# Four column tiles of 32 in place of two of 64 in the query and output products of a cross-attention kernel

## The chip, the cores and the metric

The kernel runs on one core of a Trainium2 chip. The metric is the device time of one execution in microseconds. Before the change it is 565.37 us, the median of three runs (564.01, 565.37, 566.51).

## The reference

Eight sequences of 256 tokens with 1024 features attend to eight contexts of 256 tokens, with 32 heads of 32 features. All data is 32-bit floating point.

```
x  = (hidden - mean) * rsqrt(var + 1e-5) * gamma + beta
Q  = split_heads(x @ Wq.T)
K  = V = split_heads(ctx)
scores = where(mask, Q K^T / sqrt(32), -inf)
attn   = merge_heads(softmax(scores) V)
out    = hidden + attn @ Wout.T
```

## The kernel before, in words

The program is written out in full, with no loop on the chip: a fixed order for each engine. It goes through 64 passes (n = 0 to 63), one for each sequence and each group of four heads (128 of the 1024 features). A pass does these things on TensorE, in this order:

- the scores of the next pass, line 494: eight tiles of the array, 32 rows by 64 columns each, with 256 moving columns
- some steps of the output product of an earlier sequence
- the product of probabilities and values of the pass before the last, line 645: eight tiles of 64 rows by 32 columns, with 128 moving columns
- more steps of the output product, and the query product of a later pass or sequence.

Meanwhile VectorE, ScalarE and GpSimd work on the softmax and the transposes of a pass, and the transfers are issued by SyncE's queue.

The query product and the output product are the two large ones (1024 x 1024 weights). For the first two sequences the query product is made directly, in `make_q` and `first_q`: eight chunks of 128 features added up in PSUM, with 257, 256, 129 or 128 moving columns. For the other six, and for the output product, the kernel uses a scheme with seven products of half-size blocks, from sums and differences of blocks, instead of eight. `query_product` makes one of the seven query products of a sequence in one pass: 4 x 4 chunks with 128 moving columns. `product_steps` makes one chunk after another of the seven output products, with 512 moving columns, as the table of steps for each pass says; `end_steps` does so for the last sequence.

All of them go through the helper `product` (line 216 in the profile). It takes one chunk, a stationary operand of 128 x 128 and a moving operand of 128 rows, and issues it as two matmuls on two column tiles of the array, each with 64 columns of the stationary operand, the same moving operand and its own 64 partitions of the PSUM tile. Both tiles use all 128 rows.

An fp32 matmul of the program stands as two matmuls and two weight loads in the trace: a query product of 16 chunks, 32 matmuls of the program, is a block of 64 matmuls with 64 weight loads there. The tiles' names are pq (query product), po (output product), sc (scores) and pv (values). `K` is 32 and `NA` is 4, the number of such tiles in 128 partitions.

Of the kernel before, what the change touches and what calls it, by code (L numbers as in the profile page):

```python
# [51 lines left out]
P = 128  # L52
# [7 lines left out]
def xattn_kernel(  # L60
# [10 lines left out]
    nc = tc.nc  # L71
# [9 lines left out]
    K = 32  # L81
    NA = P // K
# [129 lines left out]

    def product(out, stationary, moving, **flags):

        for w in range(2):
            nc.tensor.matmul(  # L216
                out[ts(w, P // 2)], stationary[:, ts(w, P // 2)], moving, **flags
            )

    xnTs, mvs, rstds = {}, {}, {}  # L220

# [69 lines left out]
    def first_q(s, chunks=range(NC)):  # L291

        if s == 0:
            pqs[0] = ps_q.tile([P, 512], F32, tag="pq", name="pq_0")
        cols = ds(0, P) if s == 0 else ds(P, P + 1)
        for c in chunks:
            product(
                pqs[0][:, cols], wq[:, 0, c, :], xnT0[:, c, cols],
                start=(c == chunks[0]), stop=(c == chunks[-1]),
            )  # L300
        nc.scalar.activation(qa[:, 0, cols], pqs[0][:, cols], AF.Copy, scale=NEG_SCALE)  # L301
# [41 lines left out]
    def make_q(n, second=False, chunks=range(NC)):  # L343
        b, o = divmod(n, NQ)
        if chunks[0] == 0:
            if second:
                bank = ps_o.tile([P, 512], F32, tag="po", name=f"pq_{n}")
            else:
                bank = ps_q.tile([P, 512], F32, tag="pq", name=f"pq_{n}")
            pqs[n] = bank[:, : S + 1] if b == 0 else bank[:, :S]  # L350
        for c in chunks:
            product(
                pqs[n], wq[:, o, c, :], xnTs[b](c), start=(c == 0), stop=(c == NC - 1),
            )
# [89 lines left out]
    def query_product(b, p):  # L444
        name, which, begins = Q_PRODUCTS[p]
        if b == SPLIT and name == "A11":
            which = "B11"
        if begins:
            pqs[b] = ps_q.tile([P, NK, P], F32, tag="pq", name=f"pq_{b}_{name}")
        x_ = x_part(b, name)  # L450
        for o in range(NK):
            w = weights(which, o)
            for c in range(NK):
                product(
                    pqs[b][:, o, :], w[:, c], x_[:, c], start=begins and o + c == 0,
                    stop=c == NK - 1, skip_group_check=True,
                )
# [714 lines left out]
```

## Time and profile before

| what | value |
|---|---|
| median of three runs | 565.37 us |
| profiled execution, its own time | 565.4 us |
| span in the profile | 563.6 us |
| instructions in the span | 26534 |
| TensorE matmuls / weight loads | 10364 / 10364 |
| of them the products' (line 216) | 4148 / 4148 |
| granted TensorE clock | 1.00 |

PE is TensorE's matmuls and PEld its weight loads, which run beside the matmuls. DVE is VectorE, ACT is ScalarE, POOL is GpSimd, SP is SyncE. A row of a group gives line, engine and operation, the tile that is written and those read, rows and columns of the array's tile (`128*64`), the shape, the count, then busy time in us and mean time of one in ns, and the idle time of the engine just before such instructions, with what ended it. "issue" means that the profile finds nothing that the engine waited for. A row of a stretch gives its limits, its length, then for each engine the busy time with the count of instructions, the granted clock, the busy share of the transfer engines and the rate in GB/s. A row of a queue gives packets, megabytes and the share of the 16 transfer engines' time that its packets took. A row of the chain of waits gives start, length and what it was; a row of the timeline the same, with the count and, in brackets, the idle time of the engine before it.

### The profile page before, as it was taken

Reading aid. Unit: us, or ns where it says so; the run is one execution under the profiler, and the core shown is the slowest. Engines: PE = TensorE matmul, PEld = TensorE weight load, DVE = VectorE, ACT = ScalarE, POOL = GpSimd, SP = SyncE. Lnnn points to the kernel's source line nnn. Section 1 sums busy time; section 2 is a strip of 40 time slices with the busy share of each in tenths; the row PEclk is TensorE's granted clock in tenths of the full one; section 3 lists DMA queues with packets and bytes.
Section 4 is the critical chain, followed back from the end, with each engine's and each line's share of the span. In section 5 each row is a group of like instructions: output and inputs, shape, how many; then the busy total and the mean of one; then the engine's idle time right before and its main releaser. Section 6 shows DMA issues by size and latency. Waiting matters only on the chain.

```text
span 563.6 us, 26534 instructions
## 1 busy us (share of the span) xinstructions
PE 556.2 (99%) x10364; PEld 350.8 (62%) x10364; DVE 467.4 (83%) x1716; ACT 423.4 (75%) x1464; POOL 394.8 (70%) x636
## 2 busy tenths in 40 slices
PE   8999999999999999999999999998999999999997
PEld 8666664666656667566765676566765767644443
DVE  5979889999997988888898888986878878879923
ACT  3699998898768867787777977777767776869920
POOL 2688887899786675876569665776658657448780
PEclk9999999999999999999999999999999999999999
DMA  8967657966798767887779668786667874536751
GB/s 302 396 187 208 168 158 213 305 199 168 226 299 248 217 181 197 259 249 222 196 223 283 204 185 232 237 263 174 166 168 251 260 207 135 153 101 184 208 170 74
DMA packets 47244, 119.43 MB, mean 212 GB/s; under 512 B 8976, under 2 KB 9744, under 8 KB 47120
## 3 DMA queue, kind: packets, MB, share of 16 engines
q1 hardware_dynamic: 46976, 117.74, 69.8%
q8 instruction: 82, 1.34, 1.0%
q14 instruction: 42, 0.34, 0.2%
q10 hardware_dynamic: 144, 0.01, 0.0%
HBM read 66.33 MB, written 11.53 MB: 138 GB/s over the span
## 4 chain that ended last, share of the span: by engine, by line
PE 77%; DVE 6%; POOL 6%; DMA 5%; SPq 2%; issue 2%; ACT 2%; DVEq 0%; POOLq 0%
PE po_S L216 17%; PE pq_A L216 16%; PE pv L645 10%; PE sc L494 9%; PE po_A L216 8%; PE pq L216 6%; PE pq_S L216 6%; PE po_end L216 3%; DVE pT L558 2%; DMA pT<-pT 2%; DMA r<-in_x_dram 2%; ACT e L537 1%; POOL e L552 1%; DVE e L533 1%; PE po_last L216 1%
## 5 line engine op out<-in xcount | busy, mean ns | idle before, releaser
L552 POOL TENSOR_SCALAR e<-e,rden 128x256 f32<-128x256 f32 x466 | 215.4, 479 | 119.8 <-DVE rden L544 116.9
L537 ACT ACTIVATE e<-e,mn 128x256 f32<-128x256 f32 x512 | 254.1, 502 | 41.7 <-DVE mn L533 41.3
L558 DVE STREAM_TRANSPOSE pT<-e 128x512 f32<-128x512 f32 x256 | 179.0, 704 | 35.6 <-POOL e L552 26.9
L533 DVE CUSTOM_DVE_ANT_0 e<-sc,mb 128x256 f32<-128x256 f32 x512 | 185.3, 416 | 22.0 <-PE sc L494 21.4
L564 ACT COPY pc<-pT 128x512 f32<-128x512 f32 x128 | 78.9, 617 | 54.7 <-DVE pT L558 35.2
L537 ACT ACTIVATION_READ_ACCUMULATOR e<-e,mn 128x1 f32 x512 | 98.2, 192 | 0.0
L645 PE MATMUL pv<-pT,v 64*32 64x128 f32 x4096 | 74.4, 274 | 0.4 <-DMA pT<-pc 0.4
L216 PE MATMUL po_S<-wo,at 128*64 128x512 f32 x304 | 73.9, 599 | 0.0
L645 PEld LDWEIGHTS pv<-pT,v 64*32 64x32 f32 x4096 | 57.0, 105 | 26.6 <-ACT pc L564 10.8
L494 PE MATMUL sc<-k,qa 32*64 32x256 f32 x2048 | 72.1, 387 | 0.2 <-ACT qa L301 0.2
L494 PEld LDWEIGHTS sc<-k,qa 32*64 32x64 f32 x2048 | 37.6, 131 | 49.2 <-issue 33.0
L216 PE MATMUL po_A<-wo,at 128*64 128x512 f32 x256 | 58.6, 599 | 0.0
L216 PE MATMUL pq<-xnT,wq 128*64 128x256 f32 (+3 forms) x544 | 58.4, 369 | 0.0
L216 PEld LDWEIGHTS pq_A<-xnT,wq 128*64 128x64 f32 x832 | 46.6, 137 | 7.1 <-issue 5.7
L216 PE MATMUL po_S<-wo,s 128*64 128x512 f32 x208 | 49.8, 600 | 0.7 <-DVE r L771 0.7
L216 PEld LDWEIGHTS pq<-xnT,wq 128*64 128x64 f32 x544 | 36.8, 136 | 19.1 <-issue 1.7
L216 PE MATMUL pq_A<-xnT,wq 128*64 128x128 f32 x832 | 47.8, 273 | 0.0
L544 DVE RECIPROCAL rden<-den 128x2 f32<-128x2 f32 x256 | 38.3, 150 | 7.3 <-ACT e L537 6.2
L533 DVE DVE_READ_ACCUMULATOR2_ANT mn<- 128x1 f32 x512 | 42.6, 83 | 0.0
L216 PEld LDWEIGHTS po_A<-wo,at 128*64 128x64 f32 x256 | 16.9, 136 | 30.0 <-issue 28.7
L762 POOL TENSOR_TENSOR r<-r,p 128x512 f32<-128x512 f32 x24 | 30.8, 1282 | 6.8 <-DMA r<-in_x_dram 4.4
L216 PEld LDWEIGHTS po_S<-wo,at 128*64 128x64 f32 x304 | 20.3, 136 | 21.9 <-issue 21.6
(100 smaller groups left out, 646.1 us busy)
## 6 DMA issues: line engine op xcount, KB each, us to landing
v<-in_kv_dram SPq DMA_DIRECT2D x32, 512.0 KB, 4.8
pT<-pT SPq DMA_DIRECT2D x128, 128.0 KB, 3.2
pT<-pc SPq DMA_DIRECT2D x128, 128.0 KB, 4.1
ring<-kept_T SPq DMA_DIRECT2D x20, 512.0 KB
k<-in_kv_dram SPq DMA_DIRECT2D x32, 256.0 KB, 3.8
x<-in_x_dram SPq DMA_DIRECT2D x15, 512.0 KB, 5.6
r<-in_x_dram SPq DMA_DIRECT2D x28, 256.0 KB, 4.5
out_dram<-r SPq DMA_DIRECT2D x28, 256.0 KB, 2.6
```

The costliest lines, as they stand in the source:

```text
L216: nc.tensor.matmul(out[ts(w, P // 2)], stationary[:, ts(w, P // 2)], moving, **flags)
L494: nc.tensor.matmul(scs[n][j][ts(w, P // 2), s, :], qa[r, n % NQ, ds(s * P + w * P // 2, P // 2)], ks[n - n % 2][r, n % 2, :], start=True, ...
L533: nc.vector.tensor_tensor_reduce(out=e[:, s, :], in0=pss[j][:, s, :], in1=mbs[n // NQ], scale=1.0, scalar=NO_SCORE, op0=ALU.add, op1=ALU.m ...
L537: nc.scalar.activation(e[:, s, :], e[:, s, :], AF.Exp, bias=mn[:, s : s + 1], scale=-1.0, accum_out=den[:, s : s + 1],)
L544: nc.vector.reciprocal(rden, dens[j])
L552: engine.tensor_scalar(es[j][:, s, :], es[j][:, s, :], rden[:, s : s + 1], 1.0, ALU.mult, ALU.mult,)
L558: nc.vector.transpose(pT[:, :, :, j, :, :].rearrange("p a i s k -> p (a i) s k"), es[j].rearrange("p s (b t) -> p b s t", t=K),)
L564: nc.scalar.copy(pc[:, :, ts(j, 2)], pT[:, 1, :, ts(j, 2)])
L645: nc.tensor.matmul(pvs[n][r][j * HD : (j + 1) * HD], vs[n - n % 2][ts(r, 2 * K), i, ds(n % 2 * P + j * HD, HD)], pT[ts(r, 2 * K), :, i, j, ...
L762: nc.gpsimd.tensor_tensor(r, r, p1s[b], ALU.add)
```

## The change

`product` issues one chunk as four matmuls on four column tiles of 32 columns in place of two on tiles of 64. Each takes 32 columns of the stationary operand, the same moving operand of 128 rows, and writes its own 32 partitions of the same PSUM tile. The flags that start and stop the accumulation are the same. Everything that calls `product` changes with it; scores and values, which have tiles of their own, stay as they are, and nothing changes place on any engine.

```diff
     def product(out, stationary, moving, **flags):
 
-        for w in range(2):
-            nc.tensor.matmul(
-                out[ts(w, P // 2)], stationary[:, ts(w, P // 2)], moving, **flags
-            )
+        for w in range(NA):
+            nc.tensor.matmul(out[ts(w, K)], stationary[:, ts(w, K)], moving, **flags)
```

In TensorE's order around the first of the query products with half-size blocks, each row stood so before (line, instruction, tiles, rows of the output by moving columns, count as matmuls of the program):

```order
L645 MATMUL pv_1_1883<-pT_1473,v_1540 32x128
L216 MATMUL po_A_1783<-wo,at_1_1345 64x512 x2
L216 MATMUL pq_S_1918<-sx,ring 64x128 x32
L216 MATMUL po_S_2030<-wo,s_0_1856 64x512 x4
L494 MATMUL sc_0_2040<-k_1709,qa 64x256 x2
```

and stands so now:

```order
L643 MATMUL pv_1_2169<-pT_1713,v_1780 32x128
L216 MATMUL po_A_2063<-wo,at_1_1569 32x512 x4
L216 MATMUL pq_S_2206<-sx,ring 32x128 x64
L216 MATMUL po_S_2350<-wo,s_0_2142 32x512 x8
L492 MATMUL sc_0_2364<-k_1981,qa 64x256 x2
```

The order of the blocks is the same; the products' rows have half the width and twice the count, and the numbers of lines after the helper are two lower.

## The prediction

> **What bounds the kernel now.** I read the busy shares first, then the chain of waits, then the stretch of the chain around one pass.
>
> ```profile
> PE 556.2 (99%) x10364; PEld 350.8 (62%) x10364; DVE 467.4 (83%) x1716; ACT 423.4 (75%) x1464; POOL 394.8 (70%) x636
> PE 77%; DVE 6%; POOL 6%; DMA 5%; SPq 2%; issue 2%; ACT 2%; DVEq 0%; POOLq 0%
> 0.00:564.00 564.00, 411.93 (x4148) 245.60 (x4148) 1.00 0.71 212
> 310.76 1.87 PE po_S L216 x8
> 312.63 3.49 PE pq_S L216 x64
> 316.12 1.72 PE po_S L216 x8
> 317.84 1.05 PE sc L494 x32
> 318.89 1.09 PE pv L645 x64
> 319.98 0.57 PE po_S L216
> ```
>
> TensorE is busy 99% and carries the chain; the third row (the stretch view, line 216 alone: time, PE, PEld, clock 1.00) gives the products 412 of its 556 us and 4148 of its 10364 matmuls, each with one weight load. What lengthens TensorE lengthens the kernel almost one for one.
>
> The chain rows give the pace. 64 matmuls of 128 columns last 3.49 us: 109 ns for each two. Eight of 512 columns last 1.72 us: 430 ns for each two. So both column tiles stream at once, and the time is that of the columns streamed, 0.84 ns each. The value products (pv, eight tiles of 64x32) need 1.09 us for eight rounds of 128 columns with the change of array shape and the first load inside. Since 109 and 430 ns stand in the ratio of the columns, the weight loads run beside the matmuls; one can be seen only in the first round after another shape.
>
> **Part 1: does a round of four tiles cost the same?** The trace has no 128x32 tile. From below: the four tiles stream the same columns as the two, so 109 and 430 ns, and nothing is gained in the steady state. From above: the pv rows, eight tiles over four column groups, 1.09 us / 8 = 136 ns with everything in it; 27 ns in 109 is 25%, and 25% of 412 us would be +103 us. Of the 1.09 us, one shape change and load are paid once and not per round, so I take the lower bound: 0 us.
>
> **Part 2: the first load of a block.**
>
> ```profile
> L645 PEld LDWEIGHTS pv<-pT,v 64*32 64x32 f32 x4096 | 57.0, 105 | 26.6 <-ACT pc L564 10.8 <-issue 10.5 <-ACT e L537 2.7
> L216 PEld LDWEIGHTS pq_A<-xnT,wq 128*64 128x64 f32 x832 | 46.6, 137 | 7.1 <-issue 5.7 <-ACT at L658 1.1
> ```
>
> A load of 32 columns takes 105 ns, one of 64 takes 137. Products begin after another shape once in each of the 64 passes: 64 x 32 ns = -2.0 us (at least 0, if the array's other delays cover it). Against that the last tile of a round starts two tiles later than now. pv issues 128 instructions in 1.09 us, at most 8.5 ns each; two tiles more are two to four instructions, 17 to 34 ns, at the end of 64 blocks: +1.1 to +2.2 us. Parts 1 and 2 together: -1 us, between -2 and +0.2.
>
> **Part 3: the instructions themselves.** Each product matmul becomes two of half the width, with two loads: 4148 x 2 = 8296 more instructions, beside 20,728. They have to be fetched.
>
> ```profile
> q8 instruction: 82, 1.34, 1.0%
> 0.00:278.04 278.04, 275.25 (x5125) 180.95 (x5125) 241.39 (x885) 221.92 (x754) 210.46 (x317) 1.00 0.76 230
> 0.00:381.75 381.75, 378.96 (x7142) 248.88 (x7143) 332.43 (x1222) 302.92 (x1039) 282.36 (x444) 1.00 0.77 230
> 278.04 0.35 PEld L216 LDWEIGHTS po_S<-wo,s 128*64 128x64 f32 x4 [0.20 <-issue]
> 383.71 0.30 PEld L216 LDWEIGHTS pq_S<-xnT,wq 128*64 128x64 f32 x6 [1.93 <-issue]
> q8 instruction: 1, 0.02, 5.3%
> ```
>
> The first row is the queue of instruction fetches: 82 packets, 1.34 MB. That is 16 KB each, and 20,728 / 82 = 253 matmuls and loads per packet, so this queue serves TensorE. Rows two and three are stretches from the start, with the count of matmuls and loads run (PE and PEld). Rows four and five are waits of the weight loads for which the profile finds no releaser ("issue"), in the middle of product blocks. Between the two waits lie 14,285 - 10,250 = 4035 instructions, 15.96 packets: both stops are at a packet's edge. I call the instructions of one packet a page. The last row is the queue in 381.0 to 382.5, during the long wait; from 376 to 381 and from 382.5 to 384.8 it has no packet. So TensorE ran to the end of what it had, the packet was in by 382.5, and work went on 1.2 us later. At 278.04 it is the same: packet in by 276.9, resumed 1.15 us after. I take 1.3 us from landing to use (landings read to the packet).
>
> Now the turnaround: from the moment TensorE crosses one page's edge until the page after it is usable. If it is longer than the page lasts, TensorE stands still for the rest. I read it for all 82 packets (landing + 1.3 us - time at which the edge was run); the shortest, one in the middle and the longest are shown by the counts at their edges and the queue's rows for 220.4 to 221.5, 326.1 to 327.2 (the longest's is above).
>
> ```profile
> 0.00:221.83 221.83, 219.04 (x3989) 144.01 (x3991) 192.88 (x715) 179.03 (x608) 169.27 (x248) 1.00 0.75 230
> 0.00:324.95 324.95, 322.16 (x6004) 211.99 (x6006) 282.40 (x1038) 259.81 (x886) 243.44 (x376) 1.00 0.76 230
> 0.00:375.86 375.86, 373.07 (x7014) 244.72 (x7022) 327.49 (x1200) 297.03 (x1020) 279.38 (x438) 1.00 0.76 230
> q8 instruction: 1, 0.02, 5.4%
> q8 instruction: 1, 0.02, 5.5%
> 100.00:500.00 400.00, 397.57 (x7888) 261.14 (x7872) 342.11 (x1259) 306.10 (x1071) 280.76 (x463) 1.00 0.73 215
> 100.00:500.00 400.00, 300.02 (x3350) 191.66 (x3352) 1.00 0.73 215
> PE po_S L216 <- DVE r L771: 0.7, 1, 0.7
> ```
>
> Shortest 0.9 us (221.83 to 222.7: the sequencer runs ahead and had asked early), middle 3.5 us (324.95 to 328.4), longest 7.8 us (375.86 to 383.7). 16 of the 82 are over 4.5 us, with a mean of 5.8.
>
> How long does a page last? From 100 to 500 us (the rows of that stretch: all, and line 216 alone) TensorE runs 15,760 instructions in 400 us, 39.4 per us: 253 last 6.4 us. Few turnarounds are longer, and each late one must meet a short page; that is why only 2.4 us are lost now (the 1.93 and 0.20 us above, and 0.2 more). With the change, 6702 are added: 22,462 in 400 us, 56.2 per us, and a page lasts 4.5 us. Inside a query product it is worse: 64 matmuls and 64 loads in 3.49 us become 256 instructions, one whole page in 3.5 us.
>
> The sum. At 4.5 us flat, the excess of the 82 turnarounds is 16 x (5.8 - 4.5) / 82 = 0.26 us a page. The stretch holds 22,462 / 253 = 89 pages: 23 us. Pages are not alike, though: I laid the added instructions on the trace's own times, which gives 114 pages of 3.0 to 8 us, and took each length against each of the 82 turnarounds: 31 us. By the same reckoning the kernel of now would lose 4.6 us where it loses 2.4, so I scale nothing and only take off the 2.4 that are in the span already: +28 us. Nothing hides it: the waits fall on TensorE, which is the chain, and its waits for others (the largest kind is 0.7 us, the last row) are too small to absorb them. The other engines only become idler: DVE at 83% has room.
>
> Bounds of this term: with turnarounds 0.5 us shorter throughout the same sum is 20 us (18 net), with 0.5 us longer 46 us (44 net). Longer is possible, since a sequencer that has just stood still has no lead to ask early with; shorter, since a standing TensorE leaves the transfers (share 0.73) more room.
>
> The profiled execution took 565.4 us with a span of 563.6, the median of the runs is 565.37. Sum: 565.4 - 1 + 28 = 592.4, say **593 us**.
>
> **The rivals.**
> Fetches stay hidden; this one ends on the other side, no slower. Mechanism: the next packet is asked for early enough however fast the stream runs, as at 221.83, where it was in before the edge. Then parts 1 and 2 alone count: 565.4 - 1 = 564.4 us, or 563.4 with the best of part 2. For it: 2 of the 82 packets are in before their edge even now, and all stops together cost 2.4 us. Against it: 40 of the 82 turnarounds exceed the 3.5 us that a page lasts in a query product. It decides if turnarounds come out at 3 us or less nearly everywhere.
> A rule of the Trainium skill speaks for this rival: "Runtime: NRT & Kernel Launch", section "Instruction fetch mechanics", says that instructions come in 16 KiB blocks of 256, that the next is fetched while one runs, and that crossing a boundary is mostly hidden. The packets of 16 KB here agree; "mostly hidden" agrees at 6.4 us a page, but the 1.93 us at an edge does not. By that rule the end would be 564.4 us.
>
> Fetches bind throughout. Each stop takes away the lead with which the next packet is asked for. The shortest turnaround's packet moved from 220.4, 1.4 us ahead of its edge, so the lead is worth about 1 us. With every turnaround 1 us longer the same sum is 69 us, 66 net: 565.4 - 1 + 66 = 630 us. For it: the mean turnaround of 3.6 us plus 1 is over the 4.5 us of a page. Against it: the sequencer refills quickly after a stop (the packet after 383.71 was in by 385.9).
>
> Four tiles stream slower than two (read or write of four column groups with all 128 rows): up to the 136 ns of part 1, +103 us, and the fetches then hide behind the slower pace: 565.4 - 1 + 103 = 667 us. Against: pv keeps four column groups going with less than 136. That the four tiles run two by two would double 412 us and end near 975; pv's eight at once speak against it.
>
> **How the numbers follow.** The forecast, late fetches at some 10 to 55 us net, gets 0.80; fetches hidden 0.09; bound throughout 0.07; slower streaming 0.04. The range, 573 to 620 us, is the forecast with its bounds of 18 and 44 us widened by some 10 us on each side, since one execution's turnarounds stand for all; it leaves out the hidden case and the two dear ones. A measurement of this kernel tells about 0.5% (2.8 us) from no change. Slower than that: the forecast and the two dear cases, 0.91. Of the hidden case's 0.09, 0.07 is within 0.5%, and 0.02 faster, where part 2's gain is whole and the 2.4 us lost now go too.
>
> **What would show it.** Right: the instruction queue has 114 or 115 packets; the weight loads of line 216 show waits of 0.5 to 3 us with "issue" as their end, some 30 to 40 of them, most between 100 and 500 us and few after 500, where the products have 512 columns; undisturbed blocks of 128 product matmuls still last 3.49 us; loads take about 105 ns. Wrong: undisturbed product blocks that last longer (then it is the streaming), no added "issue" waits (then fetches are hidden), or waits that end on other engines.

## The result, and the profile after

The changed kernel takes 594.16 us (median of four runs, 591.32 to 604.2) against 565.94 us for the kernel before, run beside it: a ratio of 1.0455 (95% interval 1.0389 to 1.0521). It is slower by 4.5%, 28 us. The profiled execution took 593.52 us with a span of 591.2 us, 27.6 us more than the span before. (One run of the changed kernel, 604.2 us, was disturbed; the ratio is without it.)

The page of the changed kernel: busy time, the queue of instruction fetches, the chain of waits.

```profile
PE 567.4 (96%) x14512; PEld 348.4 (59%) x14512; DVE 468.5 (79%) x1716; ACT 425.4 (72%) x1464; POOL 395.3 (67%) x636
q8 instruction: 114, 1.87, 1.3%
PE 94%; issue 3%; DMA 1%; DVE 0%; POOL 0%; ACT 0%; SPq 0%; POOLq 0%
```

There are 4148 more matmuls and as many loads, and 32 more packets of instructions. VectorE, ScalarE and GpSimd do the same work in the same busy time. The chain is TensorE and "issue". The waits of TensorE's matmuls, by tile: total, times, longest.

```profile
PE pv L643 <- issue: 7.0, 7, 1.6
PE pq_S L216 <- issue: 6.1, 7, 2.3
PE pq_A L216 <- issue: 3.5, 4, 1.6
PE po_A L216 <- issue: 1.9, 2, 1.4
```

Before, the view had one such wait, of 1.7 us. It now has 21, and they strike values (pv), whose instructions the change did not touch, as well as products. These are the times for which no matmul ran at all; a stop is longer, since the matmuls under way still finish. Here is the longest, in the timeline of the changed kernel's weight loads (start, length, engine, line, what ran, and in brackets the wait ahead of it):

```profile
255.81 0.56 PEld L216 LDWEIGHTS pq_S<-xnT,wq 128*32 128x32 f32 x19
258.96 1.05 PEld L216 LDWEIGHTS pq_S<-xnT,wq 128*32 128x32 f32 x24 [2.59 <-issue]
```

Stretches of the same kernel from the start of the span that end at this stop and at three others (length, then busy time and count for matmuls, loads, VectorE, ScalarE and GpSimd, then granted clock, DMA share and GB/s):

```profile
0.00:247.24 247.24, 238.68 (x6033) 151.76 (x6033) 209.23 (x771) 192.71 (x655) 184.33 (x272) 1.00 0.74 227
0.00:256.37 256.37, 247.81 (x6287) 157.65 (x6287) 216.04 (x797) 200.59 (x680) 189.66 (x282) 1.00 0.74 226
0.00:287.03 287.03, 275.21 (x7047) 176.92 (x7048) 237.89 (x874) 220.66 (x749) 207.43 (x313) 0.99 0.72 220
0.00:294.20 294.20, 280.76 (x7173) 179.94 (x7174) 243.40 (x894) 223.22 (x756) 210.58 (x318) 0.99 0.72 219
```

The instruction queue around the longest stop, from 256.2 to 258.9 us (packets, MB, share):

```profile
q8 instruction: 1, 0.02, 3.2%
```

Between the stops lie 508, 1521 and 252 matmuls and loads: 2, 6 and 1 packets of about 253. The packet that was missing moved from 256.30 to 257.70 us, and the loads went on at 258.96.

I put the times of all packets beside those of all instructions, as for the prediction. TensorE stops at 34 page edges, each time because the packet was not yet usable; the stops add up to 29.2 us. With TensorE's semaphore instructions counted in, all 34 lie whole multiples of 256 instructions apart. Before, there were 2 with 2.2 us. That is +27.0 of the 27.6 us.

The rest of the time is as it was, but for 3.4 us behind the longest stop at half the granted clock, told of under the last heading. The chain around an undisturbed pass:

```profile
318.70 1.05 PE sc L492 x32
319.75 1.09 PE pv L643 x64
320.84 1.00 PE po_A L216 x8
321.83 3.49 PE pq_S L216 x128
325.33 1.72 PE po_S L216 x16
```

A query product of 128 matmuls lasts 3.49 us, as 64 did; 16 of 512 columns last 1.72 us, as eight did. And the last 63.6 us, where nearly all the products have 512 columns, take the same time with 25% more matmuls (stretches as above; first row: the kernel before, second: the changed kernel).

```profile
500.00:563.60 63.60, 60.71 (x902) 25.27 (x898) 41.28 (x146) 35.95 (x126) 39.56 (x66) 1.00 0.53 159
527.60:591.20 63.60, 60.71 (x1132) 23.79 (x1124) 41.40 (x147) 36.04 (x127) 39.65 (x66) 1.00 0.53 159
```

### The profile page after: what moved, and what is told of

Same layout as the page of the kernel before. It is cut to its first block, busy times and chain, and to the rows that moved or that the text cites. A ratio compares the mean times of both kernels' runs of the same rounds, so it can differ in the third digit from the quotient of the medians.

```text
span 591.2 us, 34830 instructions
## 1 busy us (share of the span) xinstructions
PE 567.4 (96%) x14512; PEld 348.4 (59%) x14512; DVE 468.5 (79%) x1716; ACT 425.4 (72%) x1464; POOL 395.3 (67%) x636
## 4 chain that ended last, share of the span: by engine, by line
PE 94%; issue 3%; DMA 1%; DVE 0%; POOL 0%; ACT 0%; SPq 0%; POOLq 0%
PE po_S L216 20%; PE pq_A L216 18%; PE pv L643 12%; PE sc L492 11%; PE po_A L216 10%; PE pq L216 9%; PE pq_S L216 8%; PE po_end L216 3%; PE po_last L216 1%; DMA x<-in_x_dram 1%; PE po_end_s L216 0%; PE px L312 0%; POOL x L892 0%; ACT e L535 0%; PE px L278 0%
## 5 line engine op out<-in xcount | busy, mean ns | idle before, releaser
L216 PE MATMUL po_S<-wo,at 128*32 128x512 f32 x608 | 75.1, 596 | 0.0
L216 PE MATMUL po_A<-wo,at 128*32 128x512 f32 x512 | 59.7, 595 | 1.9 <-issue 1.9
L216 PE MATMUL pq<-xnT,wq 128*32 128x256 f32 (+3 forms) x1088 | 58.6, 368 | 0.0
L216 PE MATMUL po_S<-wo,s 128*32 128x512 f32 x416 | 51.5, 595 | 0.2 <-issue 0.2
L216 PEld LDWEIGHTS pq_A<-xnT,wq 128*32 128x32 f32 x1664 | 46.2, 110 | 8.9 <-issue 7.7
L216 PE MATMUL pq_A<-xnT,wq 128*32 128x128 f32 x1664 | 48.4, 273 | 0.8 <-issue 0.8
L216 PEld LDWEIGHTS pq<-xnT,wq 128*32 128x32 f32 x1088 | 33.3, 109 | 22.5 <-issue 2.6
L656 ACT COPY at<-pv 128x128 f32<-128x128 f32 x128 | 26.4, 255 | 13.8 <-PE pv L643 13.8
L216 PEld LDWEIGHTS po_A<-wo,at 128*32 128x32 f32 x512 | 15.6, 109 | 33.8 <-issue 32.5
L216 PEld LDWEIGHTS po_S<-wo,at 128*32 128x32 f32 x608 | 21.4, 110 | 22.4 <-issue 21.1
```

The costliest lines, as they stand in the source:

```text
L216: nc.tensor.matmul(out[ts(w, K)], stationary[:, ts(w, K)], moving, **flags)
L656: nc.scalar.copy(ats[b, k][:, c, :, ts(r, 2), :], pv.rearrange("p a s k -> p s a k"))
```

## Experiments

The theory is that TensorE outruns its instruction fetches. The rivals are that four column tiles stream slower, or that something else in the program is held up.

**The same count of instructions with the tiles of before.** Each matmul of a product is cut along its moving columns; the tiles stay 64 columns wide.

```diff
-        for w in range(2):
-            nc.tensor.matmul(
-                out[ts(w, P // 2)], stationary[:, ts(w, P // 2)], moving, **flags
-            )
+        deep = len(moving.shape) == 3
+        width = out.shape[-1]
+        left = width // 2
+        for piece in range(2):
+            cols = slice(0, left) if piece == 0 else slice(left, width)
+            part = moving[:, 2 * piece : 2 * piece + 2] if deep else moving[:, cols]
+            own = flags if piece == 0 else {**flags, "start": False, "skip_group_check": True}
+            for w in range(2):
+                nc.tensor.matmul(
+                    out[ts(w, P // 2)][:, cols], stationary[:, ts(w, P // 2)], part, **own
+                )
```

> The products keep two column tiles of 64, but each matmul is cut in two along its moving columns (512 as 2 x 256, 128 as 2 x 64, 257 as 128 + 129), each piece with its own weight load: as many instructions as with four tiles, and the tile shape of before. Theory of late fetches: stops at page edges as with four tiles, +25 us by the same sum over pages, and 2.3 ns more for each of some 2074 added rounds, +5 us: about 595 us (583 to 615), with 114 or 115 packets in the instruction queue. More if a load of 64 columns no longer fits under 64 moving columns. Rival, four column tiles stream slower: nothing but the added rounds, 568 to 571 us.

Measured: 599.04 us, ratio 1.0561 (1.0506 to 1.0615). Of this kernel: the instruction queue on its page, two rows of its waits by tile, and one query product in its chain of waits.

```profile
q8 instruction: 114, 1.87, 1.4%
PE pv L652 <- issue: 6.2, 5, 1.7
PE pq_S L223 <- issue: 4.3, 3, 2.0
331.04 3.73 PE pq_S L223 x128
```

The count of packets is that of the changed kernel, and so are the stops: 28, with 21.5 us (+19 against before). The rest is the added rounds: a query product takes 3.73 us in place of 3.49, because two rounds of 64 columns last 116.7 ns where one of 128 lasted 109.2: 7.5 ns for each added round, and not the 2.3 that I had put in. No tile of 32 is needed for the loss; the number of instructions does it.

**One matmul on the whole array.**

```diff
-        for w in range(2):
-            nc.tensor.matmul(
-                out[ts(w, P // 2)], stationary[:, ts(w, P // 2)], moving, **flags
-            )
+        nc.tensor.matmul(out, stationary, moving, **flags)
```

> The products as one matmul on the whole array of 128 columns: 4148 instructions fewer than before, 16,580 matmuls and loads in all, some 65 packets. Theory of late fetches: a page lasts longer, the 2.2 us of stops of before go, the first load of a block is twice as long (53 ns more in 64 to 70 blocks, +3.6 us): 565 to 568 us, no stop in the weight loads over 0.2 us. Rival, narrower tiles stream slower: the whole array would gain about as much as four tiles lost, 540 us or so. Rival, loads of 128 columns don't fit under 128 moving columns: query blocks of 64 product matmuls last longer than 3.5 us, and the time rises well over 570 us.

Measured: 566.98 us, ratio 0.9997 (0.9978 to 1.0017). The instruction queue on this kernel's page, and one query product in its chain of waits:

```profile
q8 instruction: 66, 1.08, 0.8%
313.19 3.57 PE pq_S L215 x32
```

TensorE has no "issue" wait left, and the 2.2 us of stops are gone. They are spent again: the first load of a block now takes 106 ns (53 with two tiles), and a query round lasts 111.7 ns in place of 109.2, so that 32 of them take 3.57 us. It is no faster than the kernel before, and none of the runs with the whole computation is. The streaming rival needs wider tiles to stream faster, and they do not.

**Four tiles only where instructions are sparse.** `product` chooses by a flag which the main loop sets for each pass.

```diff
+        if wide[0]:
+            ...  # two tiles of 64
+            return
+        ...  # four tiles of 32
...
+        wide[0] = n in products
```

> Four column tiles in the 22 passes that hold no half-size query product (and in the start and the end), two in the 42 that do. No pass mixes shapes in its products, so no shape change is added. These passes hold 137 of the 390 us of the products' streaming. Theory of late fetches: instructions are sparse there, the sum over pages gives 3 us more than for before: 566 to 570 us. Rival, four tiles stream slower: 137/390 of the 28 us, 575 us.

Measured: 569.01 us, ratio 1.0015 (0.9982 to 1.0049), with 89 packets and 4 stops of 3.8 us together. No difference can be told, where a share of the streaming would have cost 10 us. The complement, with the flag turned round:

```diff
-        wide[0] = n in products
+        wide[0] = n not in products
```

> The complement of the run with four tiles outside the query passes: four column tiles in the 42 passes with a half-size query product, two elsewhere. Late fetches: the sum over pages is 21 us more than for before, 587 us (581 to 594). Rival, four tiles stream slower by a share of the streaming: 253/390 of 28 us would be 18 us, but then the other passes must cost 10 us, and they cost 1 to 3 us.

Measured: 589.48 us, ratio 1.0378 (1.0318 to 1.0438), with 107 packets and 23 stops of 22.0 us together. The loss sits where a page lasts shortest. Together the two kernels lose some 23 us against the kernel before, not 28; what makes the difference no run shows.

**Four tiles with fewer transfers, and two tiles with the same.** Keys and values are loaded for the first four passes alone and used again, and the kept weight sums are not loaded back. Both kernels so compute something else; their time is for comparing with each other.

```diff
     def load_k(n):
+        if n > 2:
+            ks[n] = ks[n % 4]
+            return
...
     def load_v(n):
+        if n > 2:
+            vs[n] = vs[n % 4]
+            return
...
     def load_ring(name, half):
+        return
```

> Four tiles, with transfers left out: keys and values are loaded for the first four passes alone and used again, and the kept weight sums are not loaded back (some 37 of 118 MB less; the output is another). Theory of late fetches: the turnaround of a packet falls where it queued behind these transfers, the mean from 4.3 us to 3.5 or less, and with it the stops from 29 us to 5 to 17 us: 567 to 582 us. Rival, four tiles stream slower, or the cost is the instructions' own: transfers don't matter, 590 to 595 us.

> The kernel before, two tiles, with the same transfers left out as in the run of four tiles with fewer transfers (keys and values loaded for the first four passes alone, kept weight sums not loaded back; another output). It tells how much of that run's 28 us gain is the fetches'. Late fetches: two tiles have only 2.2 us of stops and about 1 us of waits for transfers to give back, so 562 to 566 us, within 3 us of four tiles with fewer transfers. Rival, the transfers held up something else in the program too: then two tiles gain as much as four did and end near 540 us.

Measured: four tiles 565.76 us, ratio 0.9974 (0.9947 to 1.0002); two tiles 561.25 us, ratio 0.9892 (0.9847 to 0.9937). The page of four tiles with fewer transfers:

```profile
PE 556.4 (99%) x14512; PEld 341.3 (61%) x14512; DVE 468.0 (83%) x1716; ACT 424.4 (75%) x1464; POOL 395.4 (70%) x636
q1 hardware_dynamic: 34016, 78.41, 49.3%
```

With every instruction of the change still there, and a third of the transferred bytes gone, 28 of the 28 us come back (594.2 to 565.8). Two tiles gain 5 to 6 us from the same step, so some 23 are the fetches'. I had expected a smaller gain (567 to 582 us): the stops fell to 12 with 5.8 us. The two kernels end 4.5 us apart, not within 3, and two tiles end just below the 562 to 566 us expected. The difference is 5.8 us of stops in the one and none in the other, less 0.9 us by which four tiles are quicker without stops. What two tiles gained beyond their 2.2 us of stops I have not taken apart.

All runs together. The turnaround is the mean time from the last instruction before a page's edge until the next page is usable (landing + 1.3 us), so that a stop at that edge is counted in. The kernel before, run beside each, had medians of 565.9 to 567.8 us.

| kernel | packets | mean turnaround | stops | us in them | us, median |
|---|---|---|---|---|---|
| two tiles (before) | 82 | 3.6 | 2 | 2.2 | 565.9 |
| four tiles (after) | 114 | 4.3 | 34 | 29.2 | 594.2 |
| two tiles, columns cut | 114 | 4.3 | 28 | 21.5 | 599.0 |
| whole array | 66 | 3.3 | 0 | 0 | 567.0 |
| four outside query passes | 89 | 3.9 | 4 | 3.8 | 569.0 |
| four in query passes | 107 | 4.2 | 23 | 22.0 | 589.5 |
| four, fewer transfers | 114 | 3.5 | 12 | 5.8 | 565.8 |
| two, fewer transfers | 82 | 3.0 | 0 | 0 | 561.3 |

## Why the prediction was right

**Part 1, streaming: right.** 0 us was forecast, and 0 it was: the rounds of 128 and of 512 columns last what they did. The upper bound of 136 ns, from pv's whole block, was as far off as the part had said.

**Part 2, the first load: right, and seen directly.** In the 45 product blocks that hold no stop, before or after, the change makes the block 13 ns shorter (the middle half of them within 1 ns). It is the difference of a second load that starts 27 ns sooner and a last tile that starts 13 ns later. The group of loads of the output product in the changed kernel (busy time, mean ns of one, and the idle time before) shows the shape's own length:

```profile
L216 PEld LDWEIGHTS po_A<-wo,at 128*32 128x32 f32 x512 | 15.6, 109 | 33.8 <-issue 32.5
```

70 blocks x 13 ns are 0.9 us, where -1 was forecast; the two parts were 27 and 13 ns, not 32 and 17 to 34.

**Part 3, the fetches: the mechanism was right; that the sum came so near was in part luck.** Stops of +27.0 us stand against the +28 forecast. The sum was made with the turnarounds of before, and in the changed kernel they are longer. The table's 4.3 us overstates this, since it counts the stops themselves; from the first instruction behind an edge the mean is 3.5 us before and 4.0 after. By the bound given, 0.5 us more throughout should have made the sum 46 us. It did not, because the lengthening is not throughout: the long turnarounds, which cost the most, became more frequent but not longer. Over 4.5 us are 14 of 81 before, with a mean of 5.9 us and at most 7.8, and 26 of 114 after, with a mean of 5.5 and at most 7.1. Taken against the changed kernel's own pages, the turnarounds of before give 28 us of stops and those of after 31, where 29.2 were measured. The prediction gave no reason why the long ones should not lengthen, and that is the luck. Pairing every turnaround with every page also overstates: for the kernel of now it gave 4.6 where 2.2 were lost, which the prediction had noted and left as it was.

One of the two stops that the prediction showed was none. The 0.20 us at 278.04 lie at a page's edge, but they are the change of shape from values to a product, which takes 0.20 us in all 64 passes. The second stop of before is the one at 248.3 us, 0.2 us, that the prediction counted as "0.2 more".

Why the turnaround lengthens was named as a rival's reason, the lead that is lost. The packet itself moves for 1.1 us in both kernels; what grows is the time from the edge until it starts to move, in the mean 0.9 us with the whole array, 1.1 before and 1.6 after. With fewer transfers this is 0.4 us for two tiles and 0.9 for four, so the transfers are worth some 0.7 us of it in both. The table fits a lead that is a fixed number of instructions, so that it shrinks in time when they run faster: with the same transfers the turnaround is 3.3 us at 66 packets, 3.6 at 82, 3.9 at 89, 4.2 and 4.3 at 107 and 114; with fewer transfers 3.0 at 82 and 3.5 at 114. No run changes the lead alone, so this stays a fit.

**The rest of the sum.** Stops +27.0, parts 1 and 2 -0.9, together 26.1 of 27.6 us. The missing 1.5 us is one block at half clock, told of under the last heading; the prediction had no term for it.

**The rivals.** Hidden fetches failed: at each stop the packet was usable only after its edge had been run. The rule "mostly hidden" from the Trainium skill's "Runtime: NRT & Kernel Launch", section "Instruction fetch mechanics", does not hold at 4.5 us a page (34 of 114 edges were late), while at 6.4 us it nearly does (2 of 82). Fetches bound throughout did not come about, as 80 of 114 edges cost nothing. Slower streaming fell with the 3.49 us rows and the cut columns.

**The signs named.** 114 packets, as said. 34 stops, between the 30 and 40 said, but of 0.1 to 2.6 us: some 15 are shorter than the 0.5 us said, and a third strikes the instructions of values and scores and not line 216. All but three (at 52, 57 and 503 us) are in the stretch from 100 to 500 us. Loads last 109 ns.

## What to carry to other kernels

On an engine that is busy 99%, count instructions as well as the time they stream: where TensorE ran 39 matmuls and loads per us its fetches were nearly all hidden (2 of 82 page edges were late), and at some 56 per us, with the transfer engines 71% busy, 34 of 114 were late and cost 5% of the time. Splitting work over more and narrower tiles that leaves the streaming as it is can only save on the first load of a block (13 ns each here), and it doubles the products' instructions. The sign to look for is an "issue" wait of up to three us in the middle of a block, at multiples of one instruction packet, that ends 1.3 to 1.9 us after a packet of the instruction queue has landed.

## What else the runs showed of the hardware

A late page is usable 1.3 to 1.9 us after its packet's landing (33 of the 34 stops; one 1.0). The first round after another shape is longer by 26, 53 and 106 ns for tiles of 32, 64 and 128 columns: 0.83 ns for each column loaded.

After the longest stops the granted clock of TensorE was halved for a while. Two rows of the chain behind the longest stop of the changed kernel, a stretch of that kernel, and two stretches of the kernel with four tiles in query passes (the granted clock is the third figure from the end):

```profile
256.64 2.32 issue
258.96 3.41 PE pq_S L216 x43
258.92:262.33 3.41, 3.37 (x61) 3.03 (x65) 1.45 (x2) 0.00 (x0) 2.28 (x2) 0.50 0.37 88
236.34:239.75 3.41, 3.29 (x64) 2.02 (x65) 0.67 (x4) 1.28 (x6) 0.94 (x2) 0.50 0.95 257
311.43:314.84 3.41, 3.41 (x12) 1.00 (x10) 1.61 (x4) 3.25 (x14) 1.50 (x4) 0.50 1.00 314
```

The trace's starts show 14 rounds of the first block that last 213 ns in place of 109, with weight loads of 172 to 177 ns in place of 110. The block lost 1.5 us beside the stop itself. The eight traces have three such stretches ahead of the last matmul, each 3.41 us long. They follow the three longest stops of all: 2.59, 2.50 and 3.04 us from the start of the last instruction ahead to that of the first behind. After shorter stops, up to 2.2 us, the clock stayed at 1.00. No run changes the length of a stop alone, so where the limit lies, and whether the length is all that decides, is open.

After most stops one tile is out of step with the others to the end of the block. Where the clock was full, the rounds of such blocks still lasted 109 ns.
